# Two transposes on TensorE instead of VectorE and DMA, and slice tokens head by head in the two column halves of the array

## The chip, the cores and the metric

The kernel runs on one core of a Trainium2 chip. The metric is the device time in microseconds. Before the change it is 2927.76 us, the median of three runs that lie between 2927.32 and 2928.26 us. All data is float32.

## What is computed

The input x holds 32 batches of 512 tokens with 256 features. Each batch goes through two residual layers: a graph network with two attentions, and a feed-forward layer that attends over 64 learned slices in 8 heads. Cut to what matters here:

```python
# graph network, on the layer norm of x
out = relu(xn @ mlp1_w + mlp1_b);  residual = out                 # 512 features
out = elu(gat(out, None, W_fc, a_fc)) + residual
out = relu(out @ mlp2_w + mlp2_b); residual = out                 # 256 features
out = relu(elu(gat(out, adj, W_hand, a_hand)) + residual)
x = x + out
# slice attention, on the layer norm of the new x
fx_mid = (xn @ W_fx + b_fx)  split in 8 heads of 64
slice_weights = softmax((x_mid @ W_slice + b_slice) / temp)       # per head, over 64 slices
slice_token = einsum('bhnc,bhng->bhgc', fx_mid, slice_weights)
slice_token = slice_token / (slice_weights.sum(over tokens) + 1e-5)
# attention among the 64 slice tokens of a head, spread back over the tokens, @ W_out
x = x + ...
```

`gat` is an attention whose scores are `leaky_relu(f1[i] + f2[j])`, with `elu` on its result. The first attention has no mask, the second one masks with `adj`.

## The kernel before

A batch is handled in three functions. `front` does the layer norm, the first matmul and the first attention; `middle` does the second matmul and the second attention; `back` does the slice attention. A token tile is 128 tokens (`NT` = 4 of them), a feature block 128 features (`KD` = 2 for 256 features, `KH` = 4 for 512). `NP` = 4 is the number of pairs of heads; a pair fills 128 columns.

The functions issue nothing. They talk to a `Recorder`, which takes down every operation with its engine, its reads and its writes. At the end `order` runs a list scheduler over all batches for each of 45 settings of three numbers (`ORDERS`), estimates the length of each order with costs from `_cost`, and takes the shortest; `emit` then issues that order. This is why every instruction of the profile carries line 255, that of `emit`. A batch's `front` is stage 0 and its `middle` and `back` are stage 1, so that fronts of later batches fill the gaps of earlier batches' backs. Each engine runs its queue in the order given.

PSUM is divided in eight tiles: five named `mm` for matmuls, two named `tr` for transposes and one named `sm` for small results.

A matmul contracts over the partitions, so its inputs must have the features on the partitions. Transposes bring them there, and before the change there are two kinds. Most are done by TensorE against the identity `ident`, four at a time into a `tr` tile that ScalarE or VectorE copies out; `transpose_features` does this for the second layer norm. Two are done in another way: those of the first layer norm's result `xn` (to `xnT`) and of the first attention's result `u` (to `o1T`). There `flip` lets VectorE transpose blocks of 32x32 into a stage tile, and `gather` writes the stage to a DRAM tile `scr` with four DMAs and reads it back with one, all on SyncE's queue. The token columns then stand in the order (a, t, i) in place of (t, a, i), with `a` the block of 32 in a tile and `t` the tile. `in_order` and `as_gathered` describe the same columns in the other order: matmuls that read `xnT` and `o1T` walk through them in runs of 32, and write PSUM through the view `p (t a i) -> p t a i`. The residual `o0T` is added to `o1T` block by block after the gather.

In `back` the slice tokens are not computed from `fx_mid`. The weights `w` are first contracted with the layer norm's result over the tokens (`s1`, divided by the sum of the weights), `s1` is transposed to `s1T`, and `W_fx` is applied afterwards. For each pair of heads `p` and feature block `k` one matmul of 128 columns of `wfx` against 128 columns of `s1T` gives a 128x128 block of which the two 64x64 blocks on the diagonal are wanted. The bias comes from one matmul of `bfx` (4 rows) against `nrow` (4 by 512), a row of sums put on a diagonal. `diagonal` then copies the two wanted halves from PSUM to `tok`, one by VectorE and one by ScalarE:

```python
pm = mm_tile([P, NP, P])
...
nc.tensor.matmul(pm, bfx, nrow, start=False, stop=True)
...
diagonal(lambda s: tok[ts(s, C), :, :], lambda s: pm[ts(s, C), :, ts(s, G)])
```

`tok` is read by the attention among the slices (`wqk`, `qbd`, `tokbd`) that follows.

Of the kernel before, what the change touches and what calls it, by code (L numbers as in the profile page):

```python
# [15 lines left out]
P = 128  # L16
# [4 lines left out]
class Recorder:  # L21
# [13 lines left out]

    def _region(self, ap):


        if ap.space == bass.MemoryType.PSUM:
            return 0, P, 1  # L40
        if ap.space == bass.MemoryType.DRAM:
            parts, first, start, rest = 1, 0, ap.offset, ap.ap
        else:
            (pitch, parts), *rest = ap.ap
            first, start = divmod(ap.offset, pitch)
        unit = 128 if ap.space == bass.MemoryType.DRAM else 64
        starts, run = [start], 1
        for step, count in rest:
            if step == 1:
                run = count  # L50
            elif step:
                starts = [s + step * i for s in starts for i in range(count)]
        bits = 0
        for s in starts:
            for w in range(s // unit, (s + run - 1) // unit + 1):
                bits |= 1 << w
        return first, first + parts, bits

    def take(self, engine, method, args, kwargs):
        outs, ins = list(args[:1]), [x for x in args[1:] if isinstance(x, bass.AP)]  # L60
        for key, x in kwargs.items():
            if isinstance(x, bass.AP):
                (outs if key in ("out", "accum_out") else ins).append(x)
        op = _Op(engine, method, args, kwargs, self.age, self.stage, len(self.ops))
        op.cost, op.lag = self._cost(op, outs[0], ins)
        before = {}
        for aps, writes in ((ins, False), (outs, True)):
            for ap in aps:
                if not hasattr(ap.tensor, "tag"):
                    continue  # L70
                lo, hi, bits = self._region(ap)
                log = self.logs.setdefault(ap.tensor.name, _Log(ap, self.age))
                op.logs.add(log)
                kept = []
                for entry in log.entries:
                    other, olo, ohi, obits, owrites = entry
                    if other is op:
                        kept.append(entry)
                        continue
                    if (writes or owrites) and olo < hi and lo < ohi and obits & bits:  # L80
                        before[other.index] = other
                    if not (writes and lo <= olo and ohi <= hi and not obits & ~bits):
                        kept.append(entry)
                kept.append((op, lo, hi, bits, writes))
                log.entries = kept
        for other in before.values():
            other.after.append(op)
        self.ops.append(op)

    def _cost(self, op, out, ins):  # L90


        def words(ap):
            return ap.size() // ap.ap[0][1]

        n = words(out)
        if op.method == "dma_start":
            return 0.1, 2.5 + out.size() * 4 / 180e3
        if op.engine == "tensor":
            one = max(n / 1200 + 0.002, 0.109)  # L100
            return (one if op.method == "transpose" else 2 * one), self.DRAIN
        if op.engine == "scalar":
            pointers = sum(isinstance(op.kwargs.get(k), bass.AP) for k in ("bias", "scale"))
            return 0.06 + n / 1200 + 0.09 * pointers + 0.19 * ("accum_out" in op.kwargs), 0.12
        if op.engine == "vector":
            n = max([n] + [words(x) for x in ins])
            single = op.method in ("tensor_copy", "tensor_scalar")
            fast = single and all(x.space != bass.MemoryType.PSUM for x in ins)
            pointers = sum(words(x) == 1 for x in ins) if n > 1 else 0
            return 0.07 + n / (1920 if fast else 960) + 0.065 * pointers, 0.1  # L110
        if n < 16:
            return (0.1 if op.method == "memset" else 0.3 if op.method == "tensor_scalar" else 1.1), 0.1
        return 0.2 + n / (480 if op.method == "tensor_tensor" else 960), 0.1
# [178 lines left out]
def adj_ffn_kernel(  # L292
# [40 lines left out]
    sbuf = ctx.enter_context(tc.tile_pool(name="sbuf", bufs=1))  # L333
    psum = ctx.enter_context(tc.tile_pool(name="psum", bufs=1, space=bass.MemoryType.PSUM))

    dram = ctx.enter_context(tc.tile_pool(name="dram", bufs=1, space=bass.MemoryType.DRAM))

    def ts(i, n=P):
        return slice(i * n, (i + 1) * n)

# [8 lines left out]

    def sm_tile(shape):  # L350
        return psum.tile(shape, F32, tag="sm", name="sm", bufs=1)

    Q = 32

    def flip(src, stage, t):

        nc.vector.transpose(
            stage[:, :, ts(t, Q)], src.rearrange("p (c i) -> p c i", i=Q)
        )

    def gather(stage, dst):


        blocks = stage.shape[1]
        scr = dram.tile([blocks, Q, P // Q, P], F32, name="scr", tag=f"scr{blocks}", bufs=2)
        for a in range(P // Q):
            nc.sync.dma_start(
                scr[:, :, a, :].rearrange("c r j -> r c j"), stage[ts(a, Q), :, :]
            )
        nc.sync.dma_start(  # L370
            dst, scr.rearrange("(k c) r a j -> (c r) k (a j)", c=P // Q)
        )

    def in_order(cols):

        return cols.rearrange("p (a t i) -> p t a i", a=P // Q, t=NT)

    def as_gathered(cols):

        return cols.rearrange("p (t a i) -> p a t i", a=P // Q, t=NT)  # L380

    def med(name, shape=(P, 4, 256)):
        return new(name, shape, bufs=2, tag="med")
# [211 lines left out]
    def front(b):  # L595
# [1 line left out]
        load_x(b + 1)  # L597
        xn = new("xn", [P, NT, D])
        layernorm(xt[b], xn, "ln1")
        stage = new("xn_stage", [P, D // Q, P])  # L600
        for t in range(NT):
            flip(xn[:, t, :], stage, t)
        xnT = new("xnT", [P, KD, N])
        gather(stage, xnT)
        o0T = new("o0T", [P, KH, N], bufs=2)
        for m in range(KH):
            pm = mm_tile([P, N])
            for k in range(KD):
                nc.tensor.matmul(
                    pm.rearrange("p (t a i) -> p t a i", t=NT, i=Q), w1[:, k, ts(m)],  # L610
                    in_order(xnT[:, k, :]), start=(k == 0), stop=(k == KD - 1),
                )
            nc.scalar.activation(o0T[:, m, :], pm, AF.Relu, bias=b1[:, m : m + 1])

# [52 lines left out]
            )  # L667

        o1T = new("o1T", [P, KH, N])
        stage = new("u_stage", [P, HID // Q, P], tag="p2T")  # L670
        for i in range(NT):
            pms = [mm_tile([P, HH + 1]), mm_tile([P, HH])]
            for s, pm in enumerate(pms):
                for j in range(NT):
                    nc.tensor.matmul(
                        pm, pT[:, j, ts(i)], h[:, j, s, : HH + 1 - s],
                        start=(j == 0), stop=(j == NT - 1),
                    )
            rd = small("rd", [P, 1])
            nc.vector.reciprocal(rd, pms[0][:, HH : HH + 1])  # L680
            u, m = row("u"), row("m")
            elu_elu([(pm[:, :HH], rd, ts(s, HH)) for s, pm in enumerate(pms)], m, u)
            flip(u, stage, i)
        gather(stage, o1T)
        for m in range(KH):
            o1 = o1T[:, m, :].rearrange("p (a t i) -> p a t i", t=NT, i=Q)
            nc.vector.tensor_tensor(o1, o1, as_gathered(o0T[:, m, :]), op=OP.add)
        return o1T

    def middle(b, o1T):  # L690

        o2T = new("o2T", [P, KD, N])
        for m in range(KD):
            pm = mm_tile([P, N])
            for k in range(KH):
                nc.tensor.matmul(
                    pm.rearrange("p (t a i) -> p t a i", t=NT, i=Q), w2[:, k, ts(m)],
                    in_order(o1T[:, k, :]), start=(k == 0), stop=(k == KH - 1),
                )
            nc.scalar.activation(o2T[:, m, :], pm, AF.Relu, bias=b2[:, m : m + 1])  # L700
        h = new("h2", [P, NT, D + 2])
# [66 lines left out]
    def back(b, x1):  # L768
# [48 lines left out]
        for k in range(KD):  # L817
# [4 lines left out]

        pn = sm_tile([NP, P])
        nc.tensor.transpose(pn, s1[:, :, D], ident)
        nrow = new("nrow", [NP, NP, P])
        nc.vector.tensor_tensor(
            nrow, ident[:NP, :NP, None].to_broadcast([NP, NP, P]),
            pn[:, None, :].to_broadcast([NP, NP, P]), op=OP.mult,
        )


        pm = mm_tile([P, NP, P])
        for p in range(NP):
            for k in range(KD):
                nc.tensor.matmul(
                    pm[:, p, :], wfx[:, k, ts(p)], s1T[:, k, ts(p)],
                    start=(p == 0 and k == 0), stop=False,
                )
        nc.tensor.matmul(pm, bfx, nrow, start=False, stop=True)

        def diagonal(dst, src):
            nc.vector.tensor_copy(dst(0), src(0))
            nc.scalar.copy(dst(1), src(1))

        tok = new("tok", [P, NP, G])
        diagonal(lambda s: tok[ts(s, C), :, :], lambda s: pm[ts(s, C), :, ts(s, G)])
        for s in range(2):
            nc.gpsimd.tensor_copy(tokbd[ts(s, C), :, ts(s, G)], tok[ts(s, C), :, :])
        pq = mm_tile([P, NP, G])
# [119 lines left out]
```

## Time and profile before

| What | Value |
|---|---|
| Median of three runs | 2927.76 us |
| Profiled execution, its own time | 2928.26 us |
| Profiled execution, span from first to last instruction | 2926.5 us |
| Mean granted TensorE clock | 0.996 |
| Data moved by DMA | 159.34 MB, 54 GB/s over the span |
| DMAs that write `scr` (first layer norm / first attention) | 128 of 128 KB / 128 of 256 KB |
| DMAs that read `scr` (`xnT` / `o1T`) | 32 of 512 KB / 32 of 1024 KB |

The span is one execution as the hardware profiler saw it. Groups of instructions are named by the tile that they write and the tiles that they read, `out<-in`, with shapes as partitions by elements. PE is TensorE's matmuls, PEld its weight loads, DVE is VectorE, ACT ScalarE, POOL GpSimd and SP SyncE. The profile calls the residual tile `x1` just `x`, and `w1` and `w2` just `w`. A matmul on float32 leaves two records and a transpose one. Records of matmuls that follow one another overlap, so that the length of one is not the time that it adds; the distance between two starts is.

### The profile page before, as it was taken

To read this page: it belongs to the slowest core of one execution; us is meant where nothing else is said; L and a number is where in the kernel's file an instruction comes from. 1 tells how busy PE (TensorE), PEld (TensorE's weight loads), DVE (VectorE), ACT (ScalarE), POOL (GpSimd) and SP (SyncE) were. 2 spreads that over 40 slices of the span, in tenths; PEclk is the share of its full clock that TensorE was granted. 3 is DMA by queue.
4 is the path that set the end of the run, shared out by engine and by line. 5 is a ranking of instruction groups with operands and counts; after the bars stand their busy time and mean duration, and the time that the engine had idled before them with its cause. 6 is when DMAs were issued, how large, how long until landed. Compare 5 with 4: busy or idle time off the path is not lost.

```text
span 2926.5 us, 35159 instructions
## 1 busy us (share of the span) xinstructions
PE 2853.9 (98%) x13037; PEld 2187.4 (75%) x13037; DVE 1978.3 (68%) x4694; ACT 1119.3 (38%) x2182; POOL 112.8 (4%) x233
## 2 busy tenths in 40 slices
PE   3999999999999999999999999999999999999997
PEld 3777777777778777778777778777777777777775
DVE  4567776667776666776676866677766677766675
ACT  1433444333443343443333443333433334433432
POOL 1000000000000000000000000000000000000000
PEclk9999999999999999999999999999999999999998
DMA  5112220112211122211122211122201122201110
GB/s 177 44 29 65 65 65 22 52 57 65 65 53 34 44 65 65 65 44 44 44 65 65 65 36 51 44 65 65 65 26 54 51 65 65 61 19 45 43 44 15
DMA packets 185412, 159.34 MB, mean 54 GB/s; under 512 B 9109, under 2 KB 159257, under 8 KB 185241
## 3 DMA queue, kind: packets, MB, share of 16 engines
q1 hardware_dynamic: 181904, 154.96, 18.0%
q10 hardware_dynamic: 3336, 2.14, 0.3%
q8 instruction: 103, 1.69, 0.2%
q14 instruction: 69, 0.56, 0.1%
HBM read 89.96 MB, written 67.11 MB: 54 GB/s over the span
## 4 chain that ended last, share of the span: by engine, by line
PE 95%; DVE 3%; DMA 1%; ACT 0%; issue 0%; SPq 0%; POOL 0%; ACTq 0%; POOLq 0%; DVEq 0%
PE mm L255 85%; PE tr L255 9%; PE sm L255 1%; DVE w L255 1%; DVE mx L255 0%; DVE rs L255 0%; DMA wfx<-in_L_ffn_W_fx_dram 0%; DMA temp<-n_L_ffn_temperature_dram 0%; DVE m L255 0%; DVE u L255 0%; DMA scr<-xn_stage 0%; ACT m L255 0%; DMA xt<-in_x_dram 0%; DVE pT L255 0%; DVE ln_st L255 0%
## 5 line engine op out<-in xcount | busy, mean ns | idle before, releaser
L255 PE MATMUL mm<-wfc,o0T 128*128 128x257 f32 x2048 | 579.0, 381 | 0.0
L255 PE MATMUL mm<-h,pT 128*128 128x257 f32 (+1 forms) x2048 | 454.6, 378 | 0.1
L255 PEld LDWEIGHTS mm<-h,pT 128*128 128x128 f32 x2048 | 386.1, 189 | 80.5 <-issue 13.4
L255 PEld LDWEIGHTS mm<-wfc,o0T 128*128 128x128 f32 x2048 | 363.7, 190 | 53.2 <-issue 16.3
L255 PE MATMUL mm<-gg,wT 128*128 128x256 f32 x1024 | 299.5, 379 | 0.0
L255 PE MATMUL mm<-h,p2T 128*128 128x256 f32 x1024 | 290.8, 379 | 0.0
L255 PE MATMUL mm<-xnT,w 128*128 128x512 f32 x512 | 249.3, 592 | 0.0
L255 PE MATMUL mm<-xn,w 128*128 128x257 f32 x1024 | 246.4, 382 | 0.0
L255 PE MATMUL mm<-o1T,w 128*128 128x512 f32 x512 | 241.2, 592 | 0.0
L255 PE MATMUL mm<-weff,xn2T 128*128 128x512 f32 x512 | 226.7, 596 | 0.7 <-ACT xn2T L255 0.7
L255 DVE COPY h<-mm 128x257 f32<-128x257 f32 (+1 forms) x192 | 81.7, 425 | 208.2 <-PE mm L255 204.2
L255 PEld LDWEIGHTS mm<-gg,wT 128*128 128x128 f32 x1024 | 189.2, 190 | 24.0 <-ACT gg L255 0.2
L255 PEld LDWEIGHTS mm<-h,p2T 128*128 128x128 f32 x1024 | 186.6, 190 | 24.5
L255 PEld LDWEIGHTS mm<-xn,w 128*128 128x128 f32 x1024 | 186.0, 192 | 23.7 <-issue 3.3
L255 PEld LDWEIGHTS mm<-weff,xn2T 128*128 128x128 f32 x512 | 97.8, 191 | 122.9 <-issue 99.8
L255 ACT ACTIVATE m<-m 128x512 f32<-128x512 f32 x192 | 120.9, 630 | 170.7 <-DVE m L255 170.6
L255 DVE SCALAR_TENSOR_TENSOR u<-m,u 128x512 f32<-128x512 f32 x192 | 131.5, 685 | 70.3 <-ACT m L255 70.3
L255 ACT ACTIVATE u<-mm,rd 128x256 f32<-128x256 f32 x192 | 90.3, 470 | 208.0 <-PE mm L255 181.2
L255 ACT COPY h<-mm 128x257 f32<-128x257 f32 (+1 forms) x192 | 71.8, 374 | 227.2 <-PE mm L255 224.7
L255 PE MATMUL mm<-wh,o2T 128*128 128x258 f32 x512 | 155.6, 390 | 0.0
L255 ACT ACTIVATE w<-w 128x512 f32<-128x512 f32 x128 | 80.8, 631 | 187.6 <-DVE w L255 187.6
L255 ACT ACTIVATE o2T<-mm,b 128x512 f32<-128x512 f32 x64 | 44.0, 687 | 263.2 <-PE mm L255 262.9
(141 smaller groups left out, 4396.6 us busy)
## 6 DMA issues: line engine op xcount, KB each, us to landing
scr<-u_stage SPq DMA_DIRECT2D x128, 256.0 KB, 4.0
o1T<-scr SPq DMA_DIRECT2D x32, 1024.0 KB, 5.7
xt<-in_x_dram SPq DMA_DIRECT2D x32, 512.0 KB, 4.6
x<-in_x_dram SPq DMA_DIRECT2D x32, 512.0 KB, 4.1
scr<-xn_stage SPq DMA_DIRECT2D x128, 128.0 KB, 2.4
xnT<-scr SPq DMA_DIRECT2D x32, 512.0 KB, 6.4
out_dram<-x SPq DMA_DIRECT2D x32, 512.0 KB, 3.2
w<-in_L_gnn_mlp_w_dram SPq DMA_DIRECT2D x2, 512.0 KB, 6.8
```

What stands on the lines that cost most here:

```text
L255: getattr(getattr(self.nc, op.engine), op.method)(*op.args, **op.kwargs)
```

## The change

The change has two parts that are independent in the data.

First, `flip`, `gather`, `in_order`, `as_gathered`, the stage tiles and the DRAM pool go. The first layer norm's result is transposed by `transpose_features`, as the second one's is: per batch 8 transposes of 128x128 into two `tr` tiles, and two ScalarE copies to `xnT`. In the first attention each token tile of `u` is transposed by four transposes into one `tr` tile, and one VectorE addition reads that tile and `o0T` and writes `o1T`: per batch 16 transposes and 4 additions. The matmuls of `xnT` and `o1T` read plain columns.

Second, the slice tokens are computed head by head. Each matmul takes the 64 columns of `wfx` of one head and the 64 columns of `s1T` of the same head and writes 64 partitions of PSUM, even heads to partitions 0 to 63 and odd heads to 64 to 127; this places them in the lower or the upper half of the array's columns. The 8 matmuls of 128x128 become 16 of 64x64, the bias matmul becomes two of 64x256, `nrow` is built by two operations, and one VectorE copy brings `tok` from PSUM.

In `Recorder`, `_cost` gives a matmul whose output has 64 partitions a smaller cost, and the parts that tracked DRAM tiles go.

```diff
@@ Recorder._cost
         if op.engine == "tensor":
             one = max(n / 1200 + 0.002, 0.109)
+            if out.ap[0][1] == P // 2:
+                one = max(n / 2400, 0.03)
             return (one if op.method == "transpose" else 2 * one), self.DRAIN
@@ front
-        stage = new("xn_stage", [P, D // Q, P])
-        for t in range(NT):
-            flip(xn[:, t, :], stage, t)
         xnT = new("xnT", [P, KD, N])
-        gather(stage, xnT)
+        transpose_features(xn, xnT)
...
                 nc.tensor.matmul(
-                    pm.rearrange("p (t a i) -> p t a i", t=NT, i=Q), w1[:, k, ts(m)],
-                    in_order(xnT[:, k, :]), start=(k == 0), stop=(k == KD - 1),
+                    pm, w1[:, k, ts(m)], xnT[:, k, :], start=(k == 0), stop=(k == KD - 1)
                 )
...
-            flip(u, stage, i)
-        gather(stage, o1T)
-        for m in range(KH):
-            o1 = o1T[:, m, :].rearrange("p (a t i) -> p a t i", t=NT, i=Q)
-            nc.vector.tensor_tensor(o1, o1, as_gathered(o0T[:, m, :]), op=OP.add)
+            pt = tr_tile([P, KH, P])
+            for m in range(KH):
+                nc.tensor.transpose(pt[:, m, :], u[:, ts(m)], ident)
+            nc.vector.tensor_tensor(o1T[:, :, ts(i)], pt, o0T[:, :, ts(i)], op=OP.add)
@@ middle
-                    pm.rearrange("p (t a i) -> p t a i", t=NT, i=Q), w2[:, k, ts(m)],
-                    in_order(o1T[:, k, :]), start=(k == 0), stop=(k == KH - 1),
+                    pm, w2[:, k, ts(m)], o1T[:, k, :], start=(k == 0), stop=(k == KH - 1)
@@ back
-        nrow = new("nrow", [NP, NP, P])
-        nc.vector.tensor_tensor(
-            nrow, ident[:NP, :NP, None].to_broadcast([NP, NP, P]),
-            pn[:, None, :].to_broadcast([NP, NP, P]), op=OP.mult,
-        )
-
-
-        pm = mm_tile([P, NP, P])
+        nrow = new("nrow", [NP, 2, NP, G])
+        for s in range(2):
+            nc.vector.tensor_tensor(
+                nrow[:, s], ident[:NP, :NP, None].to_broadcast([NP, NP, G]),
+                pn[:, None, ts(s, G)].to_broadcast([NP, NP, G]), op=OP.mult,
+            )
+
+
+        pm = mm_tile([P, NP, G])
         for p in range(NP):
             for k in range(KD):
-                nc.tensor.matmul(
-                    pm[:, p, :], wfx[:, k, ts(p)], s1T[:, k, ts(p)],
-                    start=(p == 0 and k == 0), stop=False,
-                )
-        nc.tensor.matmul(pm, bfx, nrow, start=False, stop=True)
+                for s in range(2):
+                    head = ts(2 * p + s, C)
+                    nc.tensor.matmul(
+                        pm[ts(s, C), p, :], wfx[:, k, head], s1T[:, k, head],
+                        start=(p == 0 and k == 0), stop=False,
+                    )
+        for s in range(2):
+            nc.tensor.matmul(
+                pm[ts(s, C)], bfx[:, ts(s, C)], nrow[:, s], start=False, stop=True
+            )
...
-        diagonal(lambda s: tok[ts(s, C), :, :], lambda s: pm[ts(s, C), :, ts(s, G)])
+        nc.vector.tensor_copy(tok, pm)
```

More of the change, by code (lines that the diff above doesn't have):

```diff
@@ L40, in _region @@
             return 0, P, 1
[L41 to L46, printed above, removed]
+        (pitch, parts), *rest = ap.ap
+        first, start = divmod(ap.offset, pitch)
         starts, run = [start], 1
@@ L54, in _region @@
         for s in starts:
-            for w in range(s // unit, (s + run - 1) // unit + 1):
+            for w in range(s // 64, (s + run - 1) // 64 + 1):
                 bits |= 1 << w
@@ L68, in take @@
             for ap in aps:
-                if not hasattr(ap.tensor, "tag"):
+                if ap.space == bass.MemoryType.DRAM:
                     continue
@@ L334, in adj_ffn_kernel @@
     psum = ctx.enter_context(tc.tile_pool(name="psum", bufs=1, space=bass.MemoryType.PSUM))
-    dram = ctx.enter_context(tc.tile_pool(name="dram", bufs=1, space=bass.MemoryType.DRAM))
     def ts(i, n=P):
@@ L351, in sm_tile @@
         return psum.tile(shape, F32, tag="sm", name="sm", bufs=1)
[L353 to L358, printed above, removed]
-        )
[L361 to L368, printed above, removed]
-            )
[L370 to L380, printed above, removed]
     def med(name, shape=(P, 4, 256)):
@@ L669, in front @@
         o1T = new("o1T", [P, KH, N])
-        stage = new("u_stage", [P, HID // Q, P], tag="p2T")
         for i in range(NT):
@@ L824, in back @@
         nc.tensor.transpose(pn, s1[:, :, D], ident)
-        nrow = new("nrow", [NP, NP, P])
-        nc.vector.tensor_tensor(
-            nrow, ident[:NP, :NP, None].to_broadcast([NP, NP, P]),
-            pn[:, None, :].to_broadcast([NP, NP, P]), op=OP.mult,
-        )
-        pm = mm_tile([P, NP, P])
+        nrow = new("nrow", [NP, 2, NP, G])
[5 more added lines that the diff above has]
+        pm = mm_tile([P, NP, G])
         for p in range(NP):
             for k in range(KD):
-                nc.tensor.matmul(
-                    pm[:, p, :], wfx[:, k, ts(p)], s1T[:, k, ts(p)],
-                    start=(p == 0 and k == 0), stop=False,
-                )
-        nc.tensor.matmul(pm, bfx, nrow, start=False, stop=True)
+                for s in range(2):
[8 more added lines that the diff above has]
+            )
         def diagonal(dst, src):
```

## The prediction

> **What bounds the kernel now.** I read four views. The first is the page's busy table: TensorE against the other engines. The second is the same table for the stretch from 300 to 2700 us alone. The third is the list of groups by shape, for counts and waits. The fourth is the timeline of TensorE, for what one instruction really costs. The page and the stretch (busy us of each engine with its instructions, then the granted clock and the DMA share) say:
>
> ```profile
> PE 2853.9 (98%) x13037; PEld 2187.4 (75%) x13037; DVE 1978.3 (68%) x4694; ACT 1119.3 (38%) x2182; POOL 112.8 (4%) x233
> PE 95%; DVE 3%; DMA 1%; ACT 0%; issue 0%; SPq 0%; POOL 0%; ACTq 0%; POOLq 0%; DVEq 0%
> ...
> 300.00:2700.00 2400.00, 2400.00 (x11022) 1844.04 (x11021) 1659.14 (x3932) 946.81 (x1846) 92.09 (x189) 1.00 0.18 54
> ```
>
> In those 2400 us TensorE never rests, and its clock is full. 27 of the 32 batches pass there (the 64 bias records nrow,bfx are two per batch; 54 of them lie in the stretch), so a batch costs 2400/27 = 88.9 us, all of it TensorE. VectorE has 31% of the stretch free, ScalarE 61%, the DMA engines 82%. What is taken off these gives nothing; what is put on TensorE is paid in full, 32 times.
>
> The mean duration in the group list must not be used as a price: matmuls overlap. The price is the distance from one start to the next. These timeline lines (start, length, engine, what, records) carry it:
>
> ```profile
> 1500.14 0.60 PE L255 MATMUL tr<-ident,w 128*128 128x128 f32 x4
> 1500.57 2.33 PE L255 MATMUL mm<-xn,w 128*128 128x257 f32 x10
> 1502.74 4.45 PE L255 MATMUL mm<-o1T,w 128*128 128x512 f32 x10
> 1507.04 0.49 PE L255 MATMUL tr<-ident,s 128*128 128x128 f32 x3
> ...
> 1509.10 0.27 PE L255 MATMUL tr<-ident,s 128*128 128x128 f32 x1
> 1509.21 0.27 PE L255 MATMUL sm<-ident,s 128*4 128x128 f32 x1
> 1509.32 0.60 PE L255 MATMUL mm<-wfc,o0T 128*128 128x257 f32 x2
> ...
> 1514.11 0.61 PE L255 MATMUL mm<-s1T,wfx 128*128 128x128 f32 x4
> 1514.55 0.60 PE L255 MATMUL mm<-wfc,o0T 128*128 128x257 f32 x2
> 1515.08 1.12 PE L255 MATMUL mm<-nrow,bfx 4*128 4x512 f32 x2
> 1516.13 0.70 PE L255 MATMUL mm<-wh,o2T 128*128 128x258 f32 x2
> 1516.67 0.60 PE L255 MATMUL mm<-wfc,o0T 128*128 128x257 f32 x2
> ```
>
> Four transposes take 1500.57 - 1500.14 = 0.43 us, so 0.109 each. Ten 257-wide records take 2.17 us (0.217 each), ten 512-wide ones 4.30 (0.430). Four slice-token records take 0.44 (0.111 each). A matmul leaves two records, a transpose one (the slice tokens are 8 matmuls in each of 32 batches, and 512 records).
>
> **What the Trainium skill says.** "TensorEngine Tiling (Array Packing)", Key Properties: tiles work independently, with weight loads and matmuls of different tiles in parallel, but "Changing tiling mode (not just tile) drains the TensorE". The trace of before shows both sides of the second half. Around nrow,bfx, which has 4 rows, the records before it take 0.53 instead of 0.43, its own two 1.05 instead of 0.86, the two after it 0.54 instead of 0.43: 0.39 us for going in and out, 0.19 per change. Around the transpose to 4 columns (1509.10, 1509.21, 1509.32) every step is 0.11: a change of columns alone cost nothing there. "TensorE: Matmul & The Clock Gate", Part 3, Measured speedup vs the span model: three column tiles ran 2.38 times as fast, 79% of three. No run here shows column tiles side by side. The same page, LDWEIGHTS: its time goes with the number of columns loaded. The trace agrees in part: a 4-column load took 85 ns where 128-column ones of the same engine took 137 to 192.
>
> **The change, part by part.**
>
> *Transposes return.* Per batch 8 for the first layer norm (2 feature blocks by 4 token tiles) and 16 for the first attention's result (4 by 4): 24 x 0.109 = 2.62 us, in 32 batches 83.7 us. All of it lies on TensorE and nothing covers it.
>
> *The gathered layout goes.* The matmuls of xnT,w and o1T,w read and write in the order (a, t, i). One might expect them to get cheaper. They don't: o1T,w runs at 0.430 per 512-wide record, which is the same 0.84 ns per column as the 257-wide contiguous ones (0.217/257). Gain 0.
>
> *VectorE, SP and ScalarE.* 128 + 128 flips go (88.9 + 49.0 us of VectorE), as do 320 DMAs on SP's queue (128 + 32 + 128 + 32). The 128 additions into o1T stay, reading PSUM (nearest row w<-mm,beff, 0.664 against 0.685 now). ScalarE gets 64 copies of xnT (0.585 each as for xn2T, 37 us) and loses 32 copies of tok. nrow becomes two operations on 256 columns (nearest row sc<-sm,amax, 0.424 each, 0.85 against 0.68). All of it is covered by the standing TensorE queue. If that cover were gone, a wait of 0.5 us at each of the six new groups of four transposes would cost 6 x 0.5 x 32 = 96 us; the transposes of e, with the same chain of VectorE, ScalarE, TensorE, show 0.0 idle, so I take 0. The two transpose buffers of PSUM serve 24 fills a batch in place of 18; at 0.59 us per emptying that is 14 of 89 us on two buffers, no bound. Loads of x and stores no longer stand behind scr on SP's queue; they were hidden, gain 0.
>
> *Slice tokens.* Before: 16 records x 0.111 = 1.78 us, and the bias 0.86 plus 0.39 for its changes of mode. After: 16 matmuls of 64 columns by 64, so 32 records, and two bias matmuls of 256, so 4 records; in the built order of instructions they stand together (2, then 14; then the 2 of the bias). With no overlap between the halves the streams cost the same as before: 32 x 64 columns is 16 x 128, and 4 x 256 is 2 x 512. Gain 0 is one end. With full overlap half of 1.78 + 0.86 goes: 1.32 us a batch, 42.2 us in all, the other end. In between I take the page's 79%: a factor of 1.59 for two tiles, an estimate from that page. 2.64 x (1 - 1/1.59) = 0.98 us a batch, **31.4 us**. Against full overlap speaks that each matmul's two records come one after the other for the same half, so the halves alternate by pairs. Changes of mode: the bias keeps its two. New are three changes of columns alone per batch (into the first two matmuls, out of them, out of the fourteen). By the 4-column transpose they cost 0; by nrow,bfx 3 x 0.19 x 32 = 18.5 us. I take 0 and keep 18.5 for the range.
>
> *Start.* TensorE stands until the weights wx land:
>
> ```profile
> 42.92 1.94 PE L255 MATMUL tr<-ident,wx 128*128 128x128 f32 x8 [42.92 <-DMA wx<-in_L_ffn_W_x_dram]
> 33.17 0.41 DVE L255 TENSOR_SCALAR xn<-xt,ln_mv,ln_rstd 128x256 f32<-128x256 f32 x1
> 46.84 1.42 DVE L255 STREAM_TRANSPOSE xn_stage<-xn 128x256 f32<-128x256 f32 x4 [3.18 <-DMA scr<-xn_stage]
> 51.31 1.02 PE L255 MATMUL mm<-xnT,w 128*128 128x512 f32 x2
> ```
>
> The four xn are done at 36.4. After the change 8 transposes of xn and 7 matmuls of xnT (14 records, 6.0 us at full clock) stand ahead of the transposes of wx, and can run in the 6.5 us to 42.9, though in part before the clock is up (the eight transposes of wx took 0.22 each). I take **6 us** off, with 3 and 9 as bounds.
>
> *End.* In the last batch tok is copied by VectorE and then ScalarE (2903.29 to 2904.17, 0.88 us on the chain); one copy of 128x256 takes about 0.43. **0.4 us** off. The rest of the end's waits (layer norm, softmax) stays.
>
> *Sum.* 2926.5 + 83.7 - 31.4 - 6 - 0.4 = 2972.4 us of span. The profiled execution took 2928.26, 1.76 above its span, and the median of the runs is 2927.76, so I add 1.3: **2974 us**, 1.6% slower.
>
> **The rivals.**
>
> 1. *The halves do not overlap* (loads of one half wait for the other, or the sequence of two records per matmul keeps them in line). Nothing in the profile shows an overlap. Then 83.7 less 3 to 6 at the start: 3005 to 3008 us.
> 2. *The halves overlap, but each change of columns drains.* The skill's sentence speaks for it, the 4-column transpose against it. 2974 + 18.5 = 2992. Both ills together: about 3025; weight loads that are no longer hidden would come on top.
> 3. *Full overlap.* 2926.5 + 83.7 - 42.2 - 6 - 0.4 + 1.3 = 2963; with 9 us at the start 2960.
> 4. *Not slower: TensorE's rest is filled.* TensorE is idle for 2926.5 - 2853.9 = 72.6 us, 43 of it at the start and most of the rest after 2866. If the new order started at 33 instead of 43, and also filled 25 us of the waits at the end, with full overlap: 2963 - 4 - 25 = 2934, still 6 above. It is level only from the point where start and end together give 41.5 us (83.7 - 42.2) beside the full overlap. The last batch's chain of layer norm and softmax has no other batch to fill it; the built order ends with the same chain. Place: 2866 to 2912. It would give 2920 to 2932.
>
> **How the numbers follow.** Partial to full overlap without drains (2957 to 2985): 0.54. No overlap, no drains (2995 to 3012): 0.23. Overlap with drains (2985 to 3000): 0.12. Worse than 3014: 0.08. Not slower: 0.03. The first is likeliest, its point is 2974. The range 2955 to 3014 takes in the first three. Faster or slower here means by more than 0.2%, 5.9 us, which is about what a measurement of this kernel can tell from no change. Faster 0.02, the same 0.01, slower 0.97.
>
> **What would show it.** In the middle of the new profile TensorE stays at 100%, and its transposes number 768 more, at 0.109 from start to start. 32 records of slice tokens take about 1.1 us a batch where they stand together, the four of the bias about 0.54 beside the 0.39 of mode changes. If 64-column records start 0.055 apart, rival 1 holds; if the record next to them is 0.1 longer than its width, rival 2. TensorE's first record comes near 36 us. The prediction is wrong if TensorE shows rests in the middle, or if the transposes hide beside other matmuls.

## The result and the profile after

The changed kernel takes 2979.39 us (median of four runs, 2978.02 to 2980.36). The kernel before took 2927.54 us in the same comparison. The ratio is 1.0177, with a 95% interval of 1.0159 to 1.0194: slower by 52 us. The profiled execution took 2978.55 us, its span is 2976.8 us.

The page of the changed kernel gives busy time by engine and the chain that ended last; an answer for the stretch from 300 to 2700 us gives the same busy columns, then clock, DMA share and GB/s:

```profile
PE 2917.3 (98%) x14381; PEld 2230.9 (75%) x14381; DVE 1895.8 (64%) x4470; ACT 1143.9 (38%) x2214; POOL 112.3 (4%) x233
PE 96%; DVE 1%; issue 1%; DMA 1%; ACT 0%; SPq 0%; POOL 0%; ACTq 0%; POOLq 0%
...
300.00:2700.00 2400.00, 2400.00 (x11851) 1838.94 (x11850) 1554.46 (x3652) 948.43 (x1837) 91.47 (x186) 1.00 0.06 18
```

TensorE is still full in the middle. VectorE's busy time went down by 82.5 us and, in this stretch, the DMA share from 0.18 to 0.06; in the middle of the kernel neither gained anything. TensorE has 1344 records more: 768 transposes, 512 slice tokens, 64 of the bias.

The timeline of TensorE in the changed kernel, one batch (start, length, engine, what, records):

```profile
1549.56 1.02 PE L252 MATMUL mm<-o1T,w 128*128 128x512 f32 x2
1550.52 0.34 PE L252 MATMUL mm<-s1T,wfx 128*64 128x64 f32 x4
1550.78 0.70 PE L252 MATMUL mm<-wh,o2T 128*128 128x258 f32 x2
1551.32 0.27 PE L252 MATMUL sm<-ident,s 128*4 128x128 f32 x1
1551.52 1.03 PE L252 MATMUL mm<-s1T,wfx 128*64 128x64 f32 x28
1552.49 0.70 PE L252 MATMUL mm<-wh,o2T 128*128 128x258 f32 x2
1553.03 0.60 PE L252 MATMUL tr<-ident,ex 128*128 128x128 f32 x4
1553.56 0.65 PE L252 MATMUL mm<-nrow,bfx 4*64 4x256 f32 x4
1554.13 0.70 PE L252 MATMUL mm<-wh,o2T 128*128 128x258 f32 x2
1554.67 0.60 PE L252 MATMUL tr<-ident,ex 128*128 128x128 f32 x4
```

Two things are to be read here. First, 28 slice-token records take 0.97 us from their start to the next instruction's start. In the records' own start times every second one begins 6 to 7 ns after the one before it, and each pair 58 ns after the pair before. This reads as two halves that work side by side, fully (a run below tests it): 16 matmuls cost 16 x 0.058 = 0.93 us of streaming in place of 1.78, the bias 0.43 in place of 0.86. Second, around each group there is time that its width (the number of columns streamed) doesn't explain. Two o1T records need 0.86 and are followed after 0.96; the four slice records need two pairs, 0.12, and take 0.26; the two records of o2T behind them take 0.54 instead of 0.43. The same stands around the other fourteen matmuls and around the bias. A stretch of half-column instructions between full-size ones is called a visit below, and the switch at either end of it a change of mode: there are three visits in each batch, and each costs about 0.35 us beside its width.

Counted from the end of one full-size instruction to where the next would have been, the three visits take 0.47 + 1.17 + 0.77 = 2.41 us. Before, slices and bias took 1.78 + 0.86 + 0.39 = 3.03. Of the 2.41, streaming is 1.36 and the changes of mode 1.05.

TensorE's start in the changed kernel, from its timeline:

```profile
34.54 0.47 PE L252 MATMUL tr<-ident,xn 128*128 128x128 f32 x1 [34.54 <-DVE xn L252]
...
38.49 8.51 PE L252 MATMUL mm<-xnT,w 128*128 128x512 f32 x14
46.84 1.04 PE L252 MATMUL tr<-ident,wx 128*128 128x128 f32 x8
```

The transposes of xn come at 34.5, and the matmuls of xnT fill the time in which wx is on its way. The first of their 14 records run at half the later rate: 0.85 us from start to start for the second to the fifth, 0.43 for the last eight, so that they take 8.35 us in all instead of 6.0. TensorE's first record comes 8.4 us earlier than before, of which 1.6 us are lost again in the first 100 us.

The sum of the spans, 2976.8 - 2926.5 = 50.3 us, is then: transposes +83.5; slices and bias in 32 batches -20.7 (the batch takes 90.66 us, and 91.31 in the run below that has the transposes and not the slices); start -6.8; and a rest of -5.7 us. The rest is a balance of two things. A batch is 2.14 us longer than before (see below), 68 us in 32, which is about 5.5 more than 83.5 - 20.7; 3.6 of it lie in the eight records of qbd, which now stand together and take 0.84 us a batch instead of 0.72. The stretches near both ends are then about 11 us shorter, beside the gain at the start. After the first 100 us TensorE is idle for 23.4 us instead of 28.2. And its mean granted clock over the span is 0.998 instead of 0.996, which I estimate from these two figures at up to about 6 us.

### The profile page after: what moved, and what is told of

Read it like the earlier page. It is cut to its first block, busy times and chain, and to the rows that moved or that the text cites. A ratio compares the mean times of both kernels' runs of the same rounds, so it can differ in the third digit from the quotient of the medians.

```text
span 2976.8 us, 36937 instructions
## 1 busy us (share of the span) xinstructions
PE 2917.3 (98%) x14381; PEld 2230.9 (75%) x14381; DVE 1895.8 (64%) x4470; ACT 1143.9 (38%) x2214; POOL 112.3 (4%) x233
## 3 DMA queue, kind: packets, MB, share of 16 engines
q10 hardware_dynamic: 3336, 2.14, 0.2%
## 4 chain that ended last, share of the span: by engine, by line
PE 96%; DVE 1%; issue 1%; DMA 1%; ACT 0%; SPq 0%; POOL 0%; ACTq 0%; POOLq 0%
PE mm L252 84%; PE tr L252 11%; PE sm L252 1%; DMA wfx<-in_L_ffn_W_fx_dram 0%; DMA temp<-n_L_ffn_temperature_dram 0%; DVE w L252 0%; DMA xt<-in_x_dram 0%; DVE m L252 0%; DVE rs L252 0%; DVE u L252 0%; DVE mx L252 0%; DVE mbias L252 0%; DVE e L252 0%; DVE ln_st L252 0%; SPq L252 0%
## 5 line engine op out<-in xcount | busy, mean ns | idle before, releaser
L252 PE MATMUL mm<-h,pT 128*128 128x257 f32 (+1 forms) x2048 | 564.0, 380 | 0.9 <-DVE pT L252 0.9
L252 PE MATMUL mm<-wfc,o0T 128*128 128x257 f32 x2048 | 524.8, 380 | 0.0
L252 PEld LDWEIGHTS mm<-wfc,o0T 128*128 128x128 f32 x2048 | 378.3, 190 | 129.2 <-issue 89.7
L252 PEld LDWEIGHTS mm<-h,pT 128*128 128x128 f32 x2048 | 371.2, 190 | 44.7 <-DVE pT L252 1.1
L252 PE MATMUL mm<-xn,w 128*128 128x257 f32 x1024 | 278.2, 380 | 0.0
L252 PE MATMUL mm<-o1T,w 128*128 128x512 f32 x512 | 255.5, 592 | 0.8 <-DVE o1T L252 0.8
L252 PE MATMUL mm<-xnT,w 128*128 128x512 f32 x512 | 235.8, 604 | 0.1
L252 DVE TENSOR_SCALAR rn<-mm 128x1 f32<-128x1 f32 x128 | 19.8, 155 | 240.8 <-PE mm L252 240.8
L252 DVE TENSOR_TENSOR w<-mm,beff 128x512 f32<-128x512 f32 x128 | 84.9, 663 | 133.7 <-PE mm L252 133.7
L252 PEld LDWEIGHTS mm<-xnT,w 128*128 128x128 f32 x512 | 93.0, 192 | 97.3 <-issue 92.5
```

What stands on the lines that cost most here:

```text
L252: getattr(getattr(self.nc, op.engine), op.method)(*op.args, **op.kwargs)
```

## The experiments

All ratios are to the kernel before, run in the same comparison. "A batch" below is the mean distance between the first bias record of the third batch and that of the thirtieth: 88.52 us before, 90.66 after.

**The second part alone.** The kernel before with the new slice tokens, bias, `tok` copy and cost; the transposes stay on VectorE and DMA.

```diff
 # against the kernel before: only the parts in _cost and back of the change
-        pm = mm_tile([P, NP, P])
+        pm = mm_tile([P, NP, G])
...
-                    pm[:, p, :], wfx[:, k, ts(p)], s1T[:, k, ts(p)],
+                        pm[ts(s, C), p, :], wfx[:, k, head], s1T[:, k, head],
```

> The kernel before with the second part alone: head-by-head slice tokens, while the two transposes stay on VectorE and DMA. My theory (the halves overlap fully, and each change between full and half columns costs 0.14 to 0.20 us) reckons 2.18 us a batch for slices, bias and changes in place of 3.03, so about -27 us, less some 3 us for the qbd matmuls that stand closer: 2900 to 2907 us, ratio 0.991 to 0.993. Rival A (the slices save nothing, and what the sum of the change was missing came from the new order of the front): 2927, ratio 1.000. Rival B (the saving is my forecast's 31 us or the full 42): 2896 or 2885.

Measured: 2905.67 us, ratio 0.9922 (0.9909 to 0.9934); a batch 87.69 us. The slices do save, by 23 us, and without the transposes the kernel is faster than before. My forecast's 31 us and the full 42 are both too large. In the batches alone the saving is 0.83 us, 27 in 32; some of it is lost again near the ends.

**The first part alone.** The changed kernel with the slice tokens, bias, `tok` and cost of before.

> The changed kernel with the second part taken back: transposes on TensorE, slice tokens by pairs of heads with one bias matmul, as before the change. My theory: 83.7 us for 768 transposes, less about 7 us at the start, less up to 12 us of waits of TensorE near both ends that the trace of before shows and that of after does not: 2992 to 2997 us, ratio 1.022 to 1.024. Rival (those waits belong to the slices, or to chance of the order): 3004, ratio 1.026.

Measured: 3002.7 us, ratio 1.0255 (1.0241 to 1.0269); a batch 91.31 us. By the number the rival was right: 74 us more than before. TensorE's first record comes 9.2 us earlier. The waits that I had counted on are indeed gone in its trace from 100 to 300 us (3.2 us of TensorE beyond the widths, 8.2 before) and from 2700 to 2830 (2.8, 9.3 before), but time came in elsewhere: a batch is 2.79 us longer than before where 24 transposes account for 2.62, about 5 us in 32 batches. These waits do not belong to the slices: after the first 100 us TensorE is idle for 23.7 us here and 23.4 in the changed kernel, against 28.2 before and 34.5 in the run with the slices alone. They go with the first part. Whether the transposes themselves remove them or the order that the kernel picks with them, no run separates. The two parts add up: -23 and +74 against +52 for both.

**Both heads in one half.** The changed kernel with the even heads' place for all: the two heads of a pair are added up, and the upper half of `tok` stays zero, so this kernel leaves out the odd heads' own slice tokens.

```diff
-                        pm[ts(s, C), p, :], wfx[:, k, head], s1T[:, k, head],
-                        start=(p == 0 and k == 0), stop=False,
+                        pm[ts(0, C), p, :], wfx[:, k, head], s1T[:, k, head],
+                        start=(p == 0 and k == 0 and s == 0), stop=False,
...
-                pm[ts(s, C)], bfx[:, ts(s, C)], nrow[:, s], start=False, stop=True
+                pm[ts(0, C)], bfx[:, ts(s, C)], nrow[:, s], start=False, stop=(s == 1)
...
-        nc.vector.tensor_copy(tok, pm)
+        nc.vector.tensor_copy(tok[ts(0, C)], pm[ts(0, C)])
```

> The changed kernel with both heads of a pair written to the lower half of the columns, one after the other, and tok's upper half left at zero; the slice tokens of even and odd heads are added up, so the slice attention is not computed rightly. The same number, shape and nearly the same order of matmuls. If the saving is two halves at work side by side: 28 to 32 records at about 0.055 instead of half as many steps, and the bias at 0.86 instead of 0.43: +1.3 to +1.4 us a batch, 3021 to 3025 us, ratio 1.032 to 1.033 to before. If it comes from shorter weight loads or the smaller tok copy: as the changed kernel, 2979, ratio 1.018.

Measured: 3020.07 us, ratio 1.0320 (1.0306 to 1.0334); a batch 92.00 us, 1.34 more than the changed kernel. Its timeline:

```profile
1570.06 1.84 PE L252 MATMUL mm<-s1T,wfx 128*64 128x64 f32 x28
1571.83 0.70 PE L252 MATMUL mm<-wh,o2T 128*128 128x258 f32 x2
...
1572.90 1.07 PE L252 MATMUL mm<-nrow,bfx 4*64 4x256 f32 x4
1573.90 0.70 PE L252 MATMUL mm<-wh,o2T 128*128 128x258 f32 x2
```

The 28 records take 1.77 us where they took 0.97, the bias 1.00 where it took 0.57. In the records' own start times single records now follow one another at 58 to 59 ns, where pairs did. The weight loads are just as short here (a record of 138 ns in both) and the visits to half columns as many. So the saving comes from the two halves side by side: without it the batch is even 0.69 us longer than with the pairs of heads of before (91.31), which is about what the changes of mode cost more, 1.05 - 0.39.

**The transpose to 4 columns as a matmul.** This tests the step from which the prediction took a price of 0.

```diff
-        nc.tensor.transpose(pn, s1[:, :, D], ident)
+        nc.tensor.matmul(pn, s1[:, :, D], ident, start=True, stop=True)
...
+            if out.ap[0][1] == 4:
+                return one, self.DRAIN
```

> The kernel before with the transpose of the sums to 4 rows (sm<-ident,s, 4 columns) done by an ordinary matmul against the identity, same result, same order of all instructions. The prediction took that transpose as proof that a change of columns costs nothing. If a transpose is simply not run as a column tile and a matmul with 4 columns is: 0.11 for the second record, about 0.10 to 0.15 going in and 0.20 going out, so +13 us: 2939 to 2943, ratio 1.004 to 1.005. If a change to a 32-column tile is free and only the 64-column one costs: +3.5 us, 2931, ratio 1.001.

Measured: 2939.1 us, ratio 1.0038 (1.0025 to 1.0050); a batch 88.93 us, 0.40 more than before. The order is the one of before, instruction by instruction. Its timeline:

```profile
1515.30 0.27 PE L257 MATMUL tr<-ident,s 128*128 128x128 f32 x1
1515.51 0.38 PE L257 MATMUL sm<-ident,s 128*4 128x128 f32 x2
1515.82 0.70 PE L257 MATMUL mm<-wfc,o0T 128*128 128x257 f32 x2
1516.36 0.38 PE L257 MATMUL mm<-s1T,wfx 128*128 128x128 f32 x2
```

In front of it 0.21 instead of 0.11, itself 0.31 for two records of 0.107, behind it 0.54 instead of 0.43: the same visit as around the slices. As a transpose the same step stood in the trace of before at 0.11, 0.11, 0.11. So this matmul with 4 columns changes the mode and the transpose with 4 columns did not; the prediction read the one off the other.

**All eighteen together.** The changed kernel; the slice tokens are held back to right before the bias.

```diff
+    def _grouped(self, ops):
+        sized = lambda op: op.engine == "tensor" and op.args[0].ap[0][1] == P // 2
+        heads, out = {}, []
+        for op in ops:
+            if sized(op) and not op.kwargs["stop"]:
+                heads.setdefault(op.age, []).append(op)
+            else:
+                if sized(op):
+                    out += heads.pop(op.age, [])
+                out.append(op)
+        return out
...
-        for op in self.order():
+        for op in self._grouped(self.order()):
```

> The changed kernel, its issued order altered in one thing: the 16 slice-token matmuls of a batch are held back until right before its two bias matmuls, so that all 18 stand together. Same instructions. My theory (each change between full and half columns costs about 0.14 us going in, 0.20 us coming out): of three visits to half columns a batch one is left, with one inner change, 0.34 + 0.20 = 0.54 us a batch less, 17 us: 2962, ratio 1.012. Rival (the change of columns is free, the missing part of the saving lies in the matmuls themselves): 2979, ratio 1.018.

Measured: 2980.59 us, ratio 1.0175 (1.0161 to 1.0189). By the number the rival is right, but the timeline and the list of waits show why the gain is missing:

```profile
1550.13 0.27 PE L264 MATMUL sm<-ident,s 128*4 128x128 f32 x1
1550.63 0.70 PE L264 MATMUL mm<-wh,o2T 128*128 128x258 f32 x2 [0.23 <-ACT o2T L264]
1551.17 0.60 PE L264 MATMUL tr<-ident,ex 128*128 128x128 f32 x4
1551.70 1.15 PE L264 MATMUL mm<-s1T,wfx 128*64 128x64 f32 x32
1552.78 0.65 PE L264 MATMUL mm<-nrow,bfx 4*64 4x256 f32 x4
...
PE mm L264 <- ACT o2T L264: 7.0, 30, 0.2
```

(The last line is of the waits: us in total, times, longest.) The thirty-two slice records now run in 1.08 us, and two visits are gone. But both groups of slice tokens had stood between the last matmul of o1T and the matmul that reads the second half of o2T, and covered the time (0.69 us) in which ScalarE writes that half. That matmul now starts 0.50 us after the transpose in front of it instead of 0.11, and its own first load is no longer hidden (0.54 instead of 0.43). 0.50 us of new wait a batch against 0.54 of gain: nothing is left.

**The sixteen together where the first two stood.** The changed kernel; the 4-column transpose goes ahead of the first two, and the full-size instructions between the first and the last slice token go behind the last, with what reads their results. This keeps the cover of ScalarE's write to o2T.

> The changed kernel with the sixteen slice-token matmuls together where the first two stood, and the full-size matmul of o2T that stood between them moved behind them; the bias stays where it was. Same instructions. In the run with all eighteen together the trace shows 0.40 us a batch of new wait in front of the matmul of o2T, which the slice tokens had covered until then. If that wait ate the gain there, this order, which keeps the cover, gives the whole price of one visit to half columns: 0.34 us a batch, 11 us: 2968 to 2970, ratio 1.014. If a visit costs nothing and the trace was misread: 2979, ratio 1.018.

Measured: 2970.2 us, ratio 1.0143 (1.0126 to 1.0160); a batch 90.32 us, 0.34 less than the changed kernel, and no wait for o2T in its list of waits. Its timeline:

```profile
1544.88 1.15 PE L289 MATMUL mm<-s1T,wfx 128*64 128x64 f32 x32
1545.97 1.14 PE L289 MATMUL mm<-wh,o2T 128*128 128x258 f32 x4
1546.94 0.60 PE L289 MATMUL tr<-ident,ex 128*128 128x128 f32 x4
```

The thirty-two records take 1.09 us as in the run above, and the matmuls of o2T follow without a wait (0.97 us for four records of 0.217, the first with its load). This bears the reading of the run above out: one visit costs 0.34 us.

**More visits.** The changed kernel; the fourteen are split in 4, 4 and 6 by instructions that followed them anyway.

> The changed kernel with the fourteen slice-token matmuls split in groups of 4, 4 and 6 by full-size instructions that followed them anyway: four visits to half columns a batch for the slices instead of two. Same instructions. My theory: two more visits of 0.34 us, 22 us more: 3001, ratio 1.025. Rival: 2979, ratio 1.018.

Measured: 2997.41 us, ratio 1.0235 (1.0221 to 1.0249); a batch 91.24 us, 0.58 more for two more visits, so 0.29 each. The timeline shows a visit's edges as before:

```profile
1560.35 0.45 PE L273 MATMUL mm<-s1T,wfx 128*64 128x64 f32 x8
1560.73 0.70 PE L273 MATMUL mm<-wh,o2T 128*128 128x258 f32 x2
1561.36 0.45 PE L273 MATMUL mm<-s1T,wfx 128*64 128x64 f32 x8
1561.74 0.43 PE L273 MATMUL tr<-ident,ex 128*128 128x128 f32 x2
1562.10 0.57 PE L273 MATMUL mm<-s1T,wfx 128*64 128x64 f32 x12
```

Eight records are four pairs, 0.23, and take 0.38; the matmul between the two groups takes 0.63, where its width asks for 0.43. A visit that is followed by a transpose costs less. The two transposes from 1561.74 take 0.36 to the start of the next group, 0.14 above their width: 0.09 is the way into that group, and 0.05 is left at the first transpose, where a matmul in its place shows 0.11. The two added visits are both followed by a transpose, and 0.29 instead of 0.34 is what this makes of them.

**Two versions without the transposes.** In the first, all eighteen half-column matmuls are held together in the kernel with the second part alone, where the full-size matmul between the groups is one of o1T and waits for nothing. The second is the same with the bias contracted over 128 partitions, padded with zeros, so that it uses all rows of the array instead of 4. The cut shows the second against the first.

```diff
-    bfx = new("bfx", [NP, P])
-    nc.scalar.dma_start(bfx, b_fx.rearrange("(p f) -> p f", p=NP))
+    bfx = new("bfx", [P, P])
+    nc.gpsimd.memset(bfx, 0.0)
+    nc.scalar.dma_start(bfx[:NP], b_fx.rearrange("(p f) -> p f", p=NP))
+    nrow = new("nrow", [P, 2, NP, G])
+    nc.gpsimd.memset(nrow, 0.0)
...
-        nrow = new("nrow", [NP, 2, NP, G])
...
-                nrow[:, s], ident[:NP, :NP, None].to_broadcast([NP, NP, G]),
+                nrow[:NP, s], ident[:NP, :NP, None].to_broadcast([NP, NP, G]),
```

> The same hold in the kernel with the second part alone (transposes on VectorE and DMA), where a full-size matmul of o1T stood between the first two and the other fourteen, and the bias already followed. My theory: one visit of 0.34 us a batch less, 11 us: 2895, ratio 0.988 to 0.989. Rival: 2906, ratio 0.992.

> As the run before, and the bias contracts over all 128 partitions instead of 4: bfx and nrow are padded with rows of zeros that are set once. If a change of rows inside half columns costs like a change of columns (0.14 us), 4 to 5 us less than the run before: 2890, ratio 0.987. If only the change of columns counts: 2895, as the run before.

Measured: 2896.62 us, ratio 0.9891 (0.9877 to 0.9904), a batch 87.35 us; and 2888.96 us, ratio 0.9866 (0.9852 to 0.9879), a batch 87.20 us. One visit less is worth 0.34 us a batch here too. The change of rows inside half columns is a change of mode as well: without it a batch is 0.15 us shorter, 4.8 us in 32. The medians stand 7.7 apart; what the other 2.9 are is not shown. The timeline of the second shows the bias right behind the slices, 0.99 and 0.53 us with no edge between:

```profile
1584.27 1.15 PE L269 MATMUL mm<-s1T,wfx 128*64 128x64 f32 x32
1585.26 0.60 PE L269 MATMUL mm<-nrow,bfx 128*64 128x256 f32 x4
1585.79 1.13 PE L269 MATMUL mm<-wfc,o0T 128*128 128x257 f32 x4
```

This last kernel is the fastest of all, 39 us below the kernel before.

## Why the prediction came out as it did

The forecast was 2974 us, slower, and the measurement is 2979.39, slower. The bound was read rightly: TensorE is full in the middle, and what is put on it is paid 32 times. (The batch was read as 88.9 us from the whole stretch; from bias to bias it is 88.52, and no sum rests on the difference.) That the number came so close is in part luck. It lies in the range that the prediction gave to an overlap without drains (2957 to 2985), while what happened is an overlap with drains, to which it gave 0.12. The sign that it had named for this is there: the record next to the slices is 0.1 us longer than its width.

- *Transposes: right.* 83.7 was forecast; 768 records at 0.109 are there, and the part alone costs 74 us with the gain at the start. That "the gathered layout" costs nothing was right too: plain columns run at 0.429 per 512-wide record (median in the middle), as gathered ones did.
- *The covers on VectorE, ScalarE and SP: right.* No wait for the new copies and additions in the middle of the changed kernel's trace.
- *Slice tokens: 31.4 us forecast, 20.7 measured.* Two terms of this step were mis-sized, in opposite directions. The overlap was set at 79% by the Trainium skill's figure for three column tiles ("TensorE: Matmul & The Clock Gate", Part 3, Measured speedup vs the span model); here the halves overlap wholly, (1.78 + 0.86)/1.36 = 1.94, worth 41 us and close to the upper end of 42.2. The argument against full overlap, that a matmul's two records follow one another in the same half, did not hold: the records begin two by two all the same. The changes of mode were set at 0 and measure (1.05 - 0.39) x 32 = 21 us; the 18.5 kept for the range was the better number. The rule was on the table: the skill's "Changing tiling mode (not just tile) drains the TensorE" ("TensorEngine Tiling (Array Packing)", Key Properties) holds here for columns as it did for rows: 0.09 to 0.10 us pass before the new mode's first record. What misled was the single case in the trace that seemed to contradict it, and that case was a transpose.
- *Start: 6 us forecast, 6.8 measured*, with the first record at 34.5 and not at 36.
- *End: 0.4 us forecast, 0.45 measured.* In the last batch the matmul of `tok` and `wqk` starts 0.48 us after the copy to `tok`; before, it started 0.93 us after the first of the two copies.
- *Rest:* the balance of -5.7 us, about 11 less near the ends and 5.5 more in the middle, was not forecast. It made up for half of the miss at the slices, by luck.
- *Rivals.* "No overlap" is refuted by the run with both heads in one half. "Overlap with drains", 2992, had the mechanism right, but stood on the 79%. "Full overlap", 2963, had the overlap right and left out the changes. With full overlap and 21 us of changes the same sum gives 2963 + 21 = 2984, and less the rest of 5.7 it gives 2978. "TensorE's rest is filled": its idle time went from 72.6 to 59.5 us, 13 us less, where this rival needed 41.5 beside the full overlap.

## What to carry to other kernels

Halves of the array's columns doubled the rate of these small matmuls, but each visit to them had a price of about a third of a microsecond. So put all that runs in one mode next to one another, rows and columns alike, and count the visits in the order that is really issued. When a group of instructions is moved, look at what it had covered; a wait of the same size can come up in the gap. And a price of 0 read from a single neighbour in a trace should be checked for being the same kind of instruction.

## What the runs showed of the hardware that was not expected

- Column halves with 64-wide streams overlap wholly in float32: pairs 58 ns apart, the two of a pair 6 to 7 ns apart, weight loads included; in one half alone single records are 58 to 59 ns apart. With 256-wide streams the bias shows the same: 0.57 us against 1.00.
- A change between full and half columns costs about 0.10 us before the new mode's first record. That record's own step is then longer than its width, as if its load were not hidden: by 0.04 to 0.05 us for 64 columns and for a transpose (load records of 0.14 us), by 0.11 for a matmul with 128 columns (0.19 us). A visit is 0.34 us, 0.29 where a transpose follows it. A change of rows inside half columns costs about 0.15.
- A transpose to 4 columns does not change the mode (0.11 us a step), the same product as a matmul does (0.30 us besides its second record).
